# Four cross-attention layers on one core: denominators of the second layer by SBUF transfers, last block of the last layer in rows, and how banks and tokens are handed out

## The chip, the core and the metric

The kernel runs on one NeuronCore of a Trainium2 chip. The core has a matrix engine (TensorE, PE in the profile; its weight loads are PEld), a vector engine (VectorE, DVE), an activation engine (ScalarE, ACT), a general engine (GpSimd, POOL) and an engine that here only issues transfers (SyncE, SP). Each runs its own list of instructions in order; semaphores make one wait for another. Data lies in device memory (DRAM), in SBUF with 128 partitions, and in PSUM, eight banks of 2 KB per partition, which TensorE writes. The metric is the device time of one execution in microseconds (us), as the median of several runs.

## The reference

The input `x` has 2048 rows of 256 values, the context 1601 rows of 512. Four cross-attention layers follow each other: a masked one, a grouped one, two masked ones. Everything is float32.

```
masked layer (16 heads of 64):
  q = x @ Wq;  k = ctx @ Wk;  v = ctx @ Wv
  logits = q k^T / 8
  logits[:, tokens A] = bias -20*(1 - mask_A), tokens B alike     (added, four columns)
  x = x + softmax(logits) v @ Wo + bo
grouped layer (16 heads of 16, 4 heads of k and v):
  q = (x / rms(x) * norm_w) @ wq;  scores = q k^T / 4
  x = x + softmax(scores) v @ wo
```

## The kernel before

**Tiles.** Rows of x come in 4 batches (b) of 512, the 1601 context rows in 13 chunks (c) of up to 128. `xs` holds x transposed (256 features as 2 x 128 partitions, rows along the free side), so that it can be the moving side of projections. A masked layer has 8 blocks (n) of 2 heads, the grouped layer 4 blocks of 4 heads. A block with a batch is a unit; a unit has 13 steps, one per chunk. So there are 4 units in each block, 16 in the grouped layer and 112 in all.

**Steps.** The loop at the end goes through all steps two at a time. At one step three units are under way: one is scored (maxima are found), the one before is exponentiated (18 steps later), and its values are multiplied (20 steps later). The order of TensorE, DVE and ACT is the written one: at the end of the program every instruction of these is tied to the one before it. SP and POOL are ordered by the scheduler.

**Masked unit.** `masked_scores` computes scores transposed (keys on partitions), ACT copies them to a tile `p` in SBUF, DVE keeps a running maximum over chunks (L704). At the end of the scoring eight transposes and a reduction give the maximum of each row (L747, L748); it goes to DRAM and back, spread over all partitions (`on_all_partitions`), DVE subtracts it (L778), ACT exponentiates (L783), TensorE multiplies by v into `po` (L823), POOL adds the chunks up for the denominator (L788). `finish` sets the rest of the unit, in steps after its last value matmul: at 2 `denominators` (transposes of the sums L844, reduction L848, reciprocal L849, spread through DRAM), at 5 `divide` (POOL, L864), at 10 `project` (TensorE L872, and DVE adds to `xs`, with the bias in the last block of a layer).

**Grouped unit.** Scores are computed twice: rows first for the maxima only (`row_maxima`, L718, reduced by DVE, L731), then transposed (`scores_again`, L793) with the maximum as an extra row of q (row 16 of each quarter of 32 partitions; one column of v is 1, so that `oT` has the denominator in the same row). A step has two parts. In each, `grouped` takes two banks for maxima and two for scores, and issues maximum, score, maximum, score, which run beside each other on different rows of the array, then the values of another unit (L823). `finish` sets `denominators` at 3: four matmuls of `oT` with `den_rows` pick the denominator rows onto partitions (L853), DVE takes reciprocals (L856), the result goes to DRAM (`cols`, L655) and back spread over partitions (`by`, L658); at 5 `divide`, at 8 `project`.

**PSUM.** One bank for `po`, one (`pm`) for projections and small things, six for scores: as two pairs `s` and one pair `b` in masked stages, as six single banks `t` in the grouped one. The class `Scores` hands them out.

**Pieces.** Projections of the next block's keys and values, queries, and what `finish` sets are pieces, each with a cost. Set pieces run at their step; others fill in by a credit that each step earns.

**Start and end.** Token numbers are loaded to all partitions (L147), and DVE works out from them the order in which context rows are gathered, so that the four special rows come last (`key_order`); POOL gathers them (L258). The mask is loaded with one value per piece (L301, L302). After the last block's `project` of a batch, `rows_out` transposes `xs` back (L631), ACT and DVE copy half each (L634, L635), and two DMAs write it out.

Of the kernel before, what the change touches and what calls it, by code (L numbers as in the profile page):

```python
# [34 lines left out]
def tile_cross_attention_stack(ctx: ExitStack, tc: tile.TileContext, t: dict, out: bass.AP):  # L35
# [47 lines left out]
    NP = 22  # L83
    const = ctx.enter_context(tc.tile_pool(name="const", bufs=1))
# [15 lines left out]
    class Scores:  # L100
# [22 lines left out]
        def heads(self, three):  # L123

            if self.banks:
                return [self.banks.tile([P, 1, QB], FP, name="t") for _ in range(2)]
            self.turn += 1
            return [self.b() if three and self.turn % 3 == 0 else self.pair()]
# [13 lines left out]
    def token_numbers():  # L142

        idx = const.tile([P, NTOK], I32, name="tok_idx")
        for l, name in enumerate(masked_names):
            for s, which, queue in ((0, "A", nc.sync), (2, "B", nc.scalar)):
                queue.dma_start(  # L147
                    out=idx[:, 4 * l + s : 4 * l + s + 2],
                    in_=t[name + "token_indices_" + which]
                    .rearrange("(o s) -> o s", o=1).to_broadcast((P, 2)),  # L150
                )
        tok = const.tile([P, NTOK], FP, name="tok")
        nc.vector.tensor_copy(tok, idx)
# [144 lines left out]
    def masks_parts():  # L298
        masks = probs.tile([P, 2, NQ], FP, name="p")
        with nc.allow_non_contiguous_dma(reason="2048 values of a mask, once"):  # L300
            nc.sync.dma_start(out=masks[:, 0, :], in_=t["mask_S_fk1"].rearrange("(n p) -> p n", p=P))  # L301
            nc.sync.dma_start(out=masks[:, 1, :], in_=t["mask_S_fk0"].rearrange("(n p) -> p n", p=P))  # L302
        parts = const.tile([P, 6, NQ], FP, name="mask_parts")

        def make():
            nc.vector.tensor_scalar(masks, masks, -1.0, 1.0, ALU.mult, ALU.add)
# [59 lines left out]
    den_rows = const.tile([P, 4], FP, name="den_rows")  # L366
# [3 lines left out]
    def small_constants():  # L370
        with nc.allow_non_contiguous_dma(reason="columns of 256 values"):
            for name in masked_names:
                bo_of.append(const.tile([P, NC], FP, name="bo_" + name))
                nc.gpsimd.dma_start(out=bo_of[-1], in_=t[name + "bo"].rearrange("(k p) -> p k", p=P))
            nc.gpsimd.dma_start(out=normw, in_=t["L1_xattn_norm_w"].rearrange("(k p) -> p k", p=P))
        nc.gpsimd.memset(sel, 0.0)
        for h, r in enumerate(QUARTERS):
            nc.gpsimd.tensor_copy(den_rows[:, h : h + 1], ident[:, r + 16 : r + 17])
# [3 lines left out]
        nc.vector.tensor_reduce(one_row, den_rows, AX.X, ALU.add)  # L382
# [243 lines left out]
    def rows_out(b):  # L626
# [621 lines left out]
```

## Time and profile before

| | |
|---|---|
| median of 3 runs | 4831.26 us (4831.16 to 4831.56) |
| the profiled execution | 4829.9 us; its span 4828.2 us |
| PE busy | 4667.0 us (97%) |
| DVE busy | 3746.8 us (78%) |
| ACT busy | 3225.1 us (67%) |
| POOL busy | 2991.6 us (62%) |
| mean granted TensorE clock | 0.981 |

The profile is of one execution. A row of a timeline has the start in us from the span's start, the duration, the engine, the line of the code, what it writes and reads, and in brackets how long the engine was idle before and what ended that. The chain of waits goes back from the last instruction, at each step to what released it or to the instruction before it on its engine, so its shares say which engine's work the time consists of. The granted clock is the share of its full clock that TensorE was given; in this trace it is either 1.0 or 0.5 at any moment. A busy TensorE isn't TensorE at its peak, as the ends of matmuls are modelled.

The grouped layer's values, and with them L853, run from about 1449 to 2340 us. Its steps alternate little:

```profile
1599.74 0.40 PE L823 MATMUL po<-p,v 128*32 128x256 f32 x4
1600.07 0.18 PEld L718 LDWEIGHTS t<-kT,q 32*128 32x128 f32 x1 [0.41 <-DVE row_top L731]
...
1601.14 0.64 PE L823 MATMUL po<-p,v 128*32 128x256 f32 x8
...
1603.03 0.64 PE L823 MATMUL po<-p,v 128*32 128x256 f32 x8
...
1604.66 0.64 PE L823 MATMUL po<-p,v 128*32 128x256 f32 x8
```

These are rows of the timeline. The value matmuls of following parts start 1.89 and 1.63 us apart; between them lie the four matmuls of maxima and scores.

### The profile page before, as it was taken

The numbers are of one execution on the slowest core, as the hardware profiler recorded it, in microseconds if no ns is written. First come the engines' busy times: TensorE is split into PE (matmuls) and PEld (weight loads), VectorE is DVE, ScalarE is ACT, GpSimd is POOL, SyncE is SP. The second block draws the span as 40 slices with busy tenths as digits, with TensorE's granted clock in tenths as the row PEclk, the third lists the DMA queues.
The fourth block names the chain that finished last, engine by engine and source line by source line (L and its number), as shares of the span: only waits on it lengthen the run. The fifth ranks groups of instructions, "written<-read, shape, count | busy, mean of one in ns | idle before, by whom it ended". The sixth has DMA issues, their size and how long they took to land.

```text
span 4828.2 us, 64072 instructions
## 1 busy us (share of the span) xinstructions
PE 4667.0 (97%) x24020; PEld 1949.9 (40%) x24020; DVE 3746.8 (78%) x3766; ACT 3225.1 (67%) x4010; POOL 2991.6 (62%) x1440
## 2 busy tenths in 40 slices
PE   8999999999999999999999999999999999999996
PEld 5444444443433333343444444444444444444432
DVE  5888888888766666652678888888888888888886
ACT  5777777777545555544677777777777777777774
POOL 3777777778620000000577777777777777777787
PEclk9999999999889999998999999999999999999998
DMA  5322322222210000021232322322232222223201
GB/s 156 85 80 79 88 74 85 83 81 78 66 33 22 26 21 21 23 56 29 67 97 74 85 83 83 84 80 84 75 92 74 85 79 85 81 79 89 72 29 35
DMA packets 345990, 337.75 MB, mean 70 GB/s; under 512 B 112425, under 2 KB 301353, under 8 KB 345680
## 3 DMA queue, kind: packets, MB, share of 16 engines
q1 hardware_dynamic: 341984, 328.28, 23.8%
q8 instruction: 189, 3.10, 0.3%
q0 software_dynamic: 1152, 3.28, 0.2%
q10 hardware_dynamic: 2544, 2.10, 0.1%
q14 instruction: 121, 0.99, 0.1%
HBM read 318.76 MB, written 14.69 MB: 69 GB/s over the span
## 4 chain that ended last, share of the span: by engine, by line
PE 87%; DVE 10%; issue 1%; POOL 1%; ACT 1%; DMA 0%; POOLq 0%; ACTq 0%; DVEq 0%; SPq 0%
PE po L823 28%; PE s L687 20%; PE t L718 9%; PE pm L394 7%; PE pm L440 6%; PE s L872 4%; PE pm L464 4%; DVE ntop L748 2%; DVE rden L848 2%; PE s L844 2%; DVE xs L884 2%; PE s L747 2%; DVE top L704 1%; POOL sums L788 1%; PE t L793 1%
## 5 line engine op out<-in xcount | busy, mean ns | idle before, releaser
L788 POOL TENSOR_TENSOR sums<-sums,p 128x1024 f32<-128x1024 f32 (+1 forms) x1152 | 2726.4, 2367 | 741.0 <-ACT p L783 569.9
L699 ACT COPY p<-s 128x1024 f32<-128x1024 f32 (+1 forms) x1248 | 1234.7, 1014 | 665.7 <-PE s L687 573.5
L823 PE MATMUL po<-p,v 128*64 128x512 f32 (+3 forms) x8320 | 1506.7, 528 | 8.8 <-ACT p L783 5.8
L778 DVE TENSOR_TENSOR p<-p,b 128x1024 f32<-128x1024 f32 (+1 forms) x1248 | 1461.3, 1209 | 55.2 <-ACT b L773 52.9
L704 DVE TENSOR_TENSOR top<-s,top 128x1024 f32<-128x1024 f32 (+1 forms) x1056 | 1291.1, 1223 | 239.7 <-ACT p L699 176.7
L687 PE MATMUL s<-q,kT 64*128 64x512 f32 (+1 forms) x4992 | 1342.9, 632 | 82.9 <-DVE ntop L748 23.8
L783 ACT ACTIVATE p<-p 128x1024 f32<-128x1024 f32 (+1 forms) x1248 | 1254.8, 1057 | 49.1 <-DVE p L778 47.7
L823 PEld LDWEIGHTS po<-p,v 128*64 128x64 f32 (+3 forms) x8320 | 366.9, 126 | 1138.9 <-issue 905.4
L687 PEld LDWEIGHTS s<-q,kT 64*128 64x128 f32 (+1 forms) x4992 | 390.2, 182 | 721.1 <-issue 217.1
L805 ACT ACTIVATE p<-t 128x512 f32<-128x512 f32 (+1 forms) x760 | 413.7, 594 | 337.3 <-PE t L793 300.5
L731 DVE TENSOR_REDUCE row_top<-t 128x1 f32<-128x512 f32 x700 | 451.2, 686 | 215.7 <-PE t L793 186.6
L864 POOL TENSOR_TENSOR oT<-oT,by 128x512 f32<-128x512 f32 x112 | 142.9, 1276 | 719.4 <-DMA by<-cols 427.0
L793 PE MATMUL t<-q,kT 32*128 32x512 f32 (+1 forms) x1520 | 496.6, 656 | 0.0
L718 PE MATMUL t<-kT,q 32*128 32x512 f32 (+1 forms) x1880 | 490.1, 563 | 0.0
L394 PEld LDWEIGHTS pm<-wv,ct 128*128 128x128 f32 (+1 forms) x2600 | 300.4, 187 | 131.0 <-issue 68.4
L394 PE MATMUL pm<-wv,ct 128*128 128x128 f32 (+2 forms) x2600 | 333.3, 281 | 2.2 <-ACT v L398 0.9
L440 PE MATMUL pm<-ct,wk 128*128 128x256 f32 (+1 forms) x1344 | 314.5, 377 | 1.1 <-ACT ct L273 1.1
L748 DVE TENSOR_REDUCE ntop<-s 128x8 f32<-128x1024 f32 x96 | 117.6, 1225 | 232.8 <-PE s L747 232.8
L440 PEld LDWEIGHTS pm<-ct,wk 128*128 128x128 f32 x1344 | 230.8, 190 | 156.5 <-issue 101.0
L718 PEld LDWEIGHTS t<-kT,q 32*128 32x128 f32 x1880 | 183.7, 187 | 161.0 <-issue 94.1
L872 PE MATMUL s<-oT,wo 128*128 128x512 f32 x392 | 199.1, 631 | 15.1 <-POOL oT L864 11.1
L786 POOL COPY sums<-p 128x1024 f32<-128x1024 f32 x96 | 99.7, 1038 | 176.0 <-ACT p L783 176.0
(152 smaller groups left out, 2310.3 us busy)
## 6 DMA issues: line engine op xcount, KB each, us to landing
ct<-ctxT SPq DMA_DIRECT2D x288, 512.0 KB
xT<-xT SPq DMA_DIRECT2D x100, 512.0 KB
spread<-cols SPq DMA_DIRECT2D x96, 512.0 KB
by<-cols SPq DMA_DIRECT2D x192, 128.0 KB
xT<-xs SPq DMA_DIRECT2D x16, 512.0 KB
ct<-ctxT SPq DMA_DIRECT2D x48, 130.0 KB
wk<-in_L_xattn_Wk_dram SPq DMA_DIRECT2D x24, 256.0 KB
wv<-in_L_xattn_Wv_dram SPq DMA_DIRECT2D x24, 256.0 KB
```

The source lines that it names most:

```text
L394: nc.tensor.matmul(pv[:md, d, :f], ct(k)[:, d * P : d * P + md], wv[:, k, :], start=(k == 0), stop=(k == NCT - 1),)
L440: nc.tensor.matmul(pk, u.wk[:, k, :], ct(k), start=(k == 0), stop=(k == NCT - 1))
L687: nc.tensor.matmul(s[:m, h, :], self.u.kT[r, a : a + m], self.q[r, :], start=True, stop=(a != TAIL),)
L699: nc.scalar.copy(p[:m], s[:m])
L704: nc.vector.tensor_tensor(self.top[:m], s[:m], self.top[:m], ALU.max)
L718: nc.tensor.matmul(s[:, at : at + n], self.q[r, ts(q, P)], self.u.kT[r, a : a + n], start=True, stop=True,)
L731: nc.vector.tensor_reduce(self.top[:, of, q, k : k + 1], s, AX.X, ALU.max)
L778: nc.vector.tensor_tensor(self.p[c][:m], self.p[c][:m], self.less[:m], ALU.add)
L783: nc.scalar.activation(p[:m], p[:m], AF.Exp)
L788: nc.gpsimd.tensor_tensor(self.sums[:m], self.sums[:m], p[:m], ALU.add)
L793: nc.tensor.matmul(s[:m], self.u.kT[r, a : a + m], self.q[r, :], start=True, stop=True)
L823: nc.tensor.matmul(to, v, p, start=(c == 0 and not part), stop=(c == NT - 1 and part != 0))
```

## The change

- `Scores.heads` takes the number of kinds that are wanted at once; `grouped` asks for maxima and scores together and deals the four tiles out in turn.
- Token numbers are loaded to one partition, and a matmul with ones puts them onto all. The mask is loaded in rows and transposed by TensorE. The bias and norm columns are set to zero on DVE before their DMAs.
- In the grouped layer `den_columns` replaces the four matmuls: four DMAs take rows 16, 48, 80 and 112 of `oT` to a tile with 4 values on each of 128 partitions. They are set at step 1; `denominators` (now reciprocal and spread only) at 3, `divide` at 6, `project` at 8.
- In the last block of the last layer x is transposed into rows early (`rows_of_x`, at fixed steps), and `project_rows` computes rows of the output from `oT` (as weights) and `wo`, adds them and writes them out. The bias of the last layer is added one block earlier.
- The very last unit: POOL adds up only the first 6 chunks (`LAST_ADDED`); the others and POOL's sum are summed on TensorE by ones, onto all partitions (`self.dens`). x goes into PSUM beforehand as a matmul with the identity (`x_below`), the projection accumulates on it, and `quarters` takes reciprocal, division, projection, copy and output by quarters of 128 rows. It also runs the projection of the unit before.

```diff
-        def heads(self, three):
+        def heads(self, three, kinds=1):
             if self.banks:
-                return [self.banks.tile([P, 1, QB], FP, name="t") for _ in range(2)]
-            self.turn += 1
-            return [self.b() if three and self.turn % 3 == 0 else self.pair()]
+                tiles = [
+                    self.banks.tile([P, 1, QB], FP, name="t") for _ in range(2 * kinds)
+                ]
+                return [tiles[i::kinds] for i in range(kinds)]
...
-        idx = const.tile([P, NTOK], I32, name="tok_idx")
+        idx = probs.tile([1, NTOK], I32, name="p")
...
-                    .rearrange("(o s) -> o s", o=1).to_broadcast((P, 2)),
-                )
+                    in_=t[name + "token_indices_" + which].rearrange("(o s) -> o s", o=1),
+                )
+        row = probs.tile([1, NTOK], FP, name="p")
+        nc.vector.tensor_copy(row, idx)
+        pt = ps_m.tile([P, NTOK], FP, name="pm")
+        nc.tensor.matmul(pt, ones[:1, :], row, start=True, stop=True)
...
-            nc.sync.dma_start(out=masks[:, 0, :], in_=t["mask_S_fk1"].rearrange("(n p) -> p n", p=P))
...
+            nc.sync.dma_start(
+                out=rows[m * NQ : (m + 1) * NQ, :], in_=t[name].rearrange("(n p) -> n p", p=P)
+            )
...
+            nc.tensor.transpose(
+                pt.rearrange("p m n -> p (m n)"), rows, ident[: 2 * NQ, : 2 * NQ]
+            )
...
-    def rows_out(b):
+    def rows_of_x(b):
         pt = psum.pair((QT, C))
         for q in range(QT):
             for k in range(NC):
                 nc.tensor.transpose(pt[:, q, ts(k, P)], xs[:, b, k, ts(q, P)], ident)
...
+        x_rows_of[b] = work.tile([P, QT, C], FP, name="ct", bufs=3)
+        nc.scalar.copy(x_rows_of[b], pt)
...
-            else:
+            elif c < self.added:
                 nc.gpsimd.tensor_tensor(self.sums[:m], self.sums[:m], p[:m], ALU.add)
...
+            if self.masked and self.very_last:
+                if c == 0:
+                    self.dens = ps_m.tile([P, QB], FP, name="pm")
+                todo = [self.p[c]] if c >= self.added else []
+                if c == NT - 1:
+                    todo.append(self.sums)
+                for p in todo:
+                    k = m if p is self.p[c] else P
+                    for h in range(2):
+                        nc.tensor.matmul(
+                            self.dens[self.rows(h), :], ones[:k, :64], p[:k, h, :],
+                            start=(c == self.added), stop=(p is self.sums),
+                        )
...
             else:
-                pd = ps_m.tile([P, QT, 4], FP, name="pm")
-                for q in range(QT):
-                    nc.tensor.matmul(
-                        pd[:, q, :], self.oT[:, columns(q)], den_rows, start=True, stop=True
-                    )
-                nc.vector.reciprocal(rden, pd.rearrange("p q h -> p h q"))
+                nc.vector.reciprocal(rden, self.dens)
...
+        def den_columns(self):
+            self.dens = small.tile([P, 4, QT], FP, name="dens", bufs=1)
+            with nc.allow_non_contiguous_dma(reason="512 values, four at a time"):
+                for h, r in enumerate(QUARTERS):
+                    nc.sync.dma_start(
+                        out=self.dens[:, h, :],
+                        in_=self.oT[r + 16 : r + 17, :].rearrange("o (p q) -> o p q", q=QT),
+                    )
...
+        def project_rows(self, py=None):
+            py = py or psum.pair((QT, C))
+            for q in range(QT):
+                nc.tensor.matmul(
+                    py[:, q, :], self.oT[:, ts(q, P)], self.u.wo, start=True, stop=True
+                )
+            rows = x_rows_of[self.b]
+            nc.vector.tensor_tensor(rows, py, rows, ALU.add)
+            for q in (0, QT // 2):
+                rows_out(self.b, rows, q, QT // 2)
...
+        def quarters(self, before):
+            rden = work.tile([P, NC, QB], FP, name="xT")[:, 0, :]
+            for q in range(QT):
+                nc.vector.reciprocal(rden[:, ts(q, P)], self.dens[:, ts(q, P)])
+                nc.gpsimd.tensor_tensor(
+                    self.oT[:, ts(q, P)], self.oT[:, ts(q, P)], rden[:, ts(q, P)], ALU.mult
+                )
+            before.project_rows(psum.b().rearrange("p a (b c) -> p (a b) c", c=C))
+            rows = work.tile([P, QT, C], FP, name="ct", bufs=3)
+            for q in range(QT):
+                nc.tensor.matmul(
+                    self.py[q], self.oT[:, ts(q, P)], self.u.wo, start=False, stop=True,
+                )
+                nc.scalar.copy(rows[:, q, :], self.py[q])
+                rows_out(self.b, rows, q, 1)
...
+            if not self.masked:
+                return [
+                    (1, Piece(self.den_columns, 0.0)), (3, Piece(self.denominators, 0.0)),
+                    (6, Piece(self.divide, 0.0)), (8, Piece(self.project, 2.0, False)),
+                ]
...
+            for b, at in enumerate((2, 12, 38, NB * NT + 12)):
+                piece = Piece(lambda b=b: rows_of_x(b), 1.0, False)
+                if b == NB - 1:
+                    piece = Piece(lambda: of[len(units) - 1].x_below(), 2.0, False)
+                pieces.at(start + at, [(0, piece)])
...
-                tops = psum.heads(three) if scoring else []
-                exps = psum.heads(three) if exping else []
+                tiles = psum.heads(three, bool(scoring) + bool(exping))
+                tops = tiles.pop(0) if scoring else []
+                exps = tiles.pop(0) if exping else []
```

## The prediction

> **What bounds it now.** First the page's chain of waits that ended last: 87% of the span is TensorE, and no single line leads.
>
> ```profile
> ## 4 chain that ended last, share of the span: by engine, by line
> PE 87%; DVE 10%; issue 1%; POOL 1%; ACT 1%; DMA 0%; POOLq 0%; ACTq 0%; DVEq 0%; SPq 0%
> ```
>
> The change touches four stretches, so I read the chain for each. In the second layer (cut to 1450–2120 us) it is TensorE throughout: no other engine has more than 0.1%, and L853, the denominators' matmul, holds 3.5%:
>
> ```profile
> by line: PE t L718 52.9%; PE po L823 27.7%; PE t L793 4.8%; PE pm L576 3.7%; PE pm L853 3.5%; PE t L872 3.4%; PE pm L440 1.9%; PE pm L546 1.4%; issue 0.3%; PE pm L761 0.3%; ACT kT L550 0.1%
> ```
>
> The same chain in order of time, 1510–1532 us, has start, us and what. L853 stands between one value matmul and the next maxima, and costs TensorE 1.96 us:
>
> ```profile
> 1516.71 0.57 PE po L823 x8
> 1517.28 1.96 PE pm L853 x8
> 1519.24 0.62 PE t L718
> ```
>
> Windows around it (stretch, length, PE busy, granted clock, DMA share, GB/s) show a second price: the 4 us after it run at 0.57 of the clock.
>
> ```profile
> 1516.00:1520.00 4.00, 4.00 (x32) 1.00 0.00 0
> 1520.00:1524.00 4.00, 4.00 (x28) 0.57 0.11 15
> 1524.00:1528.00 4.00, 4.00 (x46) 1.00 0.17 56
> ```
>
> Last the chain of the end, which is a row of engines waiting for each other:
>
> ```profile
> 4806.29 2.00 PE s L844 x8
> 4808.31 1.24 DVE rden L848
> ...
> 4809.80 1.54 DMA cols<-rden
> ...
> 4811.90 3.10 DMA by<-cols
> ...
> 4816.48 3.79 PE s L872 x4
> ...
> 4821.76 1.77 PE s L631 x7
> ...
> 4824.17 0.69 DVE ct L635
> ```
>
> **Banks in turn: nothing.** In steady state one part takes TensorE 1.64 us, the next 1.89 us; the 0.26 us between are a maximum waiting for DVE to empty the bank of three maxima before. The change hands out the four banks in another order of the names. But a bank is bound at a tile's first write, in TensorE's order, and that order (maximum, score, maximum, score) stays. Built, both programs keep maxima in banks 2, 3, 4 and scores in 5, 6, 7, and each waits for the same earlier reader. I cost it at 0.
>
> **Denominators without TensorE.** Removed: 16 units x four matmuls (eight instructions each) of 1.96 us. The chain holds 23.5 us of them at 12 units (3.5% of 670 us) and 2.0 us for the one at 2258; the last (2335 us) runs into the third layer, where DVE is also late, and I don't count it: 15 x 1.96 = 29.4 us.
>
> The clock: 7 of the 16 L853 (at 1462, 1517, 1628, 1736, 1897, 2121, 2183 us) are followed within 1.9 to 3.5 us by exactly 3.4 us of half clock; otherwise TensorE is busy there. The Trainium skill ("TensorE: Matmul & The Clock Gate", What's actually happening) has free-running windows of 3.41 us and halves the clock after an idle one. By the rule as stated, L853 costs no clock, since TensorE isn't idle for a window: 29.4 us in all. By the row a window that is largely filled with 4-column matmuls counts as idle. I take the row. From L853 to L853 a unit lasts 52.2 to 54.2 us without a dip and 53.6 to 57.3 with one; I take 1.2 us a dip (half of 3.4 us less slack), 7 x 1.2 = 8.4 us.
>
> Added: four DMAs on SP per unit (2 KB each, 128 pieces of 16 bytes), from SBUF to SBUF. They wait for oT, copied at 1503.9–1504.5 us. Behind them on SP stand the next unit's xT and factor loads, the 1/denominator's own cols and by, and the top rows; xT is needed a unit (50 us) later. The reciprocal stays at step 3 of the unit after, behind that step's maxima, i.e. at about 1516.48 + 1.29 = 1517.8 us. **Cover: 13.3 us.** No row shows such a transfer; the nearest is cols<-rden, the same 16-byte pieces in one DMA:
>
> ```profile
> SPq L658 <- DMA cols<-rden: 36.4, 16, 2.8
> ```
>
> That is 36.4/16 = 2.3 us on average, 2.8 at most. Issuing four costs about 1.7 us (the four by<-cols), so they land some 4 us after oT. The skill speaks against it: "DMA: Bandwidth & Descriptors" (Rules for kernel authors) wants many small transfers coalesced, and its fixed cost is about 2 us each; served one after the other that is 8 us plus the issue, 10 us, still inside 13.3. Both give 0; the ends are 0 and a stall (third rival). Division moves from step 5 to 6 and projection stays at 8: cols and by took until 1526.3, projection came at 1542.4, so the 3.5 us later divide is hidden. The piece's cost going from 1 to 0 moves later keys' pieces forward, with the same work.
>
> **Start: 0.6 us.** Token numbers come as 8 bytes per DMA instead of 128 copies of them, landing before 7.6 us (they then waited 5.85 us); a matmul and two small copies are added. DVE's 6.5 us of index work and the first gathers move up by 2 to 3 us. But TensorE is then still transposing x: in the trace L592 ends at 20.3 us and the two halves of the first context block came at 20.26 and 21.12 us, so only about 0.8 us is there to win, less 0.2 us for the mask's transpose (L631 needs 1.09 us for eight). Ends: -1 and +2.5. The two mask DMAs with 4-byte pieces held SP 4.1 us; row loads replace them. The bias loads move from POOL's first 6 us to about 80 us, behind four DVE memsets: four issues, 3.2 us on POOL, whose next work (L786) starts at 90.85; free.
>
> **Last block: 2 us.** There DVE is the bound (busy 35.8 of 40 us; 13 subtractions and maxima of 1.21 us and five small ones make 36.4 of a unit of about 37). For x in rows, ACT copies it earlier (1.01 us) and DVE adds once (1.21) where it had two adds (1.41) and a copy (0.69): 0.9 us for each of the first two batches. TensorE's transposes and 1024 projected columns only move. The bias goes into the block before, +0.2 us of DVE under TensorE.
>
> **End: 22.5 us.** From the trace's rows:
> - The last unit's exponentials no longer wait in the middle for the copy out and for the unit before's sums after five chunks; those sums come after seven. The copy of the spread maxima is at about 4767.2 (4768.97 before: no wait of 1.9 us for L879), chunk 6's exponential ends at 4779.1 (1.12 us each), and the sums' transposes at 4779.3.
> - TensorE: values of chunks 5 and 6 (1.94), ones for 6 (0.97, as values), x into PSUM (16 instructions as L394's, 1.8), six chunks of 0.97 + 0.97 (11.6), ones for the tile into which POOL has added chunks 0 to 5 (0.97): 4796.6. POOL's six chunks are done by 4783.
> - Four reciprocals of 128x128. Not in the trace: 4 elements take 178 ns (L617), 8 take 203 (L849), so 6.3 ns an element and 0.96 us each; lower bound 0.2, an ordinary DVE pass. I take 0.96: 4800.4. Then POOL 0.45 (line through 128x512 and 128x1024), TensorE 0.48, ACT 0.37: 4801.7. The other batch's 1.93 us projection lies beneath.
> - Last copy before: 4824.86. Gain 23.2; I take 22.5 for SP's six output issues in a row. With everything at half clock, as the end is now (26 us from 4804), it would be about 11; with fast reciprocals 25.
>
> **Sum.** 29.4 + 8.4 + 0.6 + 2 + 22.5 = 63 us. Profiled execution 4829.9 (span 4828.2) → 4767; the median of the runs is 1.4 us above it: **4768 us**.
>
> **Rivals.**
> 1. Four small DMAs just fail the cover: the reciprocal holds DVE's maxima about as long as the matmul held TensorE. Then 63 - 38 = 25 us: 4806. For it: nothing measured lands 128 pieces on 128 partitions from one row. Against: 13.3 us of cover. 6%.
> 2. The turn of banks removes the 0.26 us stall in all 208 steps: 54 us more, 4714. Against: same banks in both builds. 2%.
> 3. **Slower**: the four transfers are served one at a time at the dearest row for 128 small pieces, the token loads' 5.85 us. They land at 23.4 us, DVE stands 10.1 us at the reciprocal in each of 16 units, TensorE with it: +162 - 63 = +99, 4930. It decides from a landing of 13.3 + 63/16 = 17.2 us after oT. Against: those 5.85 us lay beside 2 MB of x. 4%.
> 4. The end gains half: TensorE falls to half clock while waiting for reciprocals, or x in PSUM holds both pairs too long: 4780 to 4785. 10%, inside my range.
>
> **Numbers.** Forecast with its own spread 78%, rivals 1 to 4 as above. Upward: no clock gain (+8.4), end 11 (+11.5), start -1: 4790; toward rival 1 I go to 4803. Downward: all 16 L853 and 1.7 us a dip (-5.5), end 25, start +2.5: 4758; I go to 4750. What counts as no change is within 0.2%, about 10 us. Faster 0.93, same 0.02, slower 0.05.
>
> **What would show it.** Right: L853 gone from the second layer's chain, fewer half-clock stretches, no DVE wait at its reciprocal for dens, unit spacing near 51.5 us; steps still alternating 1.64 and 1.89 us. From the last unit's final sum on TensorE to the end about 8 us. Wrong: DVE or SP waiting on dens; the dips elsewhere instead; reciprocals far from 0.96 us.

## The result, and the profile after

| | before | after |
|---|---|---|
| median | 4831.35 us (4831.16 to 4831.56) | 4754.41 us (4745.24 to 4755.4) |
| ratio | | 0.9837 (95%: 0.9822 to 0.9853) |
| the profiled execution | 4829.9 us | 4745.2 us |
| mean granted TensorE clock | 0.981 | 0.992 |
| half clock in the span | 185 us | 72 us |

The changed kernel is 77 us faster in the median; 63 us were forecast (4768 us), and the result lies inside the range of 4750 to 4803 us. Its profiled execution is 9 us quicker than its other three, so the difference of the two profiles is 84.7 us.

The page's chain of waits, after:

```profile
## 4 chain that ended last, share of the span: by engine, by line
PE 87%; DVE 10%; issue 1%; ACT 1%; POOL 0%; DMA 0%; another core or an unknown queue 0%; ACTq 0%; DVEq 0%; POOLq 0%
```

The kernel is bound as before. The chain in the second layer (1450 to 2110 us of after) has no denominators any more (3.5% before):

```profile
by line: PE t L744 54.4%; PE po L849 28.4%; PE t L819 5.2%; PE pm L595 3.8%; PE t L920 3.5%; PE pm L459 1.9%; PE pm L565 1.4%; PE pm L413 0.8%; issue 0.3%; PE pm L787 0.3%
```

L744, L849 and L819 are the former L718, L823 and L793. Windows of 4 us around the reciprocal, which runs at 1515.6 us in after (stretch, length, PE busy, PEld, DVE, ACT, POOL busy, granted clock, DMA share, GB/s):

```profile
1512.00:1516.00 4.00, 4.00 (x40) 1.19 (x32) 2.93 (x6) 2.20 (x5) 0.00 (x0) 1.00 0.00 1
1516.00:1520.00 4.00, 4.00 (x34) 1.43 (x34) 2.58 (x4) 2.32 (x5) 0.00 (x0) 1.00 0.18 28
1520.00:1524.00 4.00, 4.00 (x42) 1.59 (x42) 2.58 (x4) 2.97 (x6) 1.27 (x1) 1.00 0.13 44
```

The clock column stays at 1.00 where it fell to 0.57 before. Rows of the timeline of after, value matmuls:

```profile
1588.11 0.64 PE L849 MATMUL po<-p,v 128*32 128x256 f32 x8
1590.00 0.64 PE L849 MATMUL po<-p,v 128*32 128x256 f32 x8
1591.64 0.64 PE L849 MATMUL po<-p,v 128*32 128x256 f32 x8
```

They still alternate 1.89 and 1.64 us: the turn of banks took no stall away. VectorE never stands at its reciprocal of the transferred denominators: the view of tile `dens` lists nothing under "sat idle".

```profile
L894 DVE RECIPROCAL rden<-dens x16: 243/243/245, 1464.3 to 2277.7; 128x16 f32<-128x16 f32 x16
its engine sat idle before it (us, times) until:
```

Last the end of after, timeline rows from the last sums by ones on:

```profile
4731.96 1.03 PE L862 MATMUL pm<-sums,ones 128*64 128x512 f32 x4
...
4733.03 3.39 DVE L961 RECIPROCAL xT<-pm 128x128 f32<-128x128 f32 x4 [7.83 <-PE pm L862]
...
4735.78 4.23 SPq L658 DMA_DIRECT2D out_dram<-ct  x6
...
4738.26 0.37 ACT L971 COPY ct<-s 128x256 f32<-128x256 f32 x1 [0.85 <-PE s L968]
```

A reciprocal of 128x128 takes 3.39 / 4 = 0.85 us (0.96 was taken); from the end of the sums to the span's end (4743.5) are 10.5 us, some 8 were forecast.

**Where the time went.** As marks I take the reduction that ends each unit's search for maxima (units from 0: 0–31 first layer, 32–47 second, 48–79 third, 80–111 last). From mark to mark, with the half clock that the trace's clock records have in between:

| from mark to mark | before | after | gain |
|---|---|---|---|
| start to unit 0 | 75.8 (0 half) | 82.3 (6.8 half) | -6.5 |
| unit 0 to 33, with the change to the second layer | 1339.6 (61.4 half) | 1334.7 (47.8 half) | 4.9 |
| 33 to 47: second layer | 786.1 (37.5 half) | 747.6 (10.2 half) | 38.5 |
| 47 to 48: change to the third layer | 87.4 (34.1 half) | 70.9 (0 half) | 16.5 |
| 48 to 107 | 2321.8 (17.1 half) | 2313.7 (3.4 half) | 8.1 |
| 107 to 111: last block | 148.1 (0 half) | 149.0 (0 half) | -0.9 |
| 111 to the end | 69.4 (34.3 half) | 45.3 (3.4 half) | 24.2 |

(Gains are taken before rounding. The 48-to-107 row loses its half clock within the first four units, as the third layer begins.)

### The profile page after: what moved, and what is told of

Read it like the earlier page. It is cut to its first block, busy times and chain, and to the rows that moved or that the text cites. A ratio compares the mean times of both kernels' runs of the same rounds, so it can differ in the third digit from the quotient of the medians.

```text
span 4743.5 us, 64047 instructions
## 1 busy us (share of the span) xinstructions
PE 4596.3 (97%) x23943; PEld 1914.1 (40%) x23943; DVE 3744.2 (79%) x3768; ACT 3226.5 (68%) x4013; POOL 2977.4 (63%) x1436
## 4 chain that ended last, share of the span: by engine, by line
PE 87%; DVE 10%; issue 1%; ACT 1%; POOL 0%; DMA 0%; another core or an unknown queue 0%; ACTq 0%; DVEq 0%; POOLq 0%
PE po L849 28%; PE s L713 20%; PE t L744 9%; PE pm L413 7%; PE pm L459 6%; PE pm L483 4%; PE s L920 4%; DVE rden L891 2%; PE s L887 2%; DVE ntop L774 2%; DVE xs L932 2%; PE s L773 2%; DVE top L730 1%; DVE p L804 1%; PE t L819 1%
## 5 line engine op out<-in xcount | busy, mean ns | idle before, releaser
L814 POOL TENSOR_TENSOR sums<-sums,p 128x1024 f32<-128x1024 f32 x1145 | 2711.0, 2368 | 736.8 <-ACT p L809 566.0
L849 PE MATMUL po<-p,v 128*64 128x512 f32 (+3 forms) x8320 | 1493.5, 522 | 4.9 <-ACT p L809 2.6
L713 PE MATMUL s<-q,kT 64*128 64x512 f32 (+1 forms) x4992 | 1336.7, 629 | 85.9 <-DVE ntop L774 23.2
L849 PEld LDWEIGHTS po<-p,v 128*64 128x64 f32 (+3 forms) x8320 | 365.7, 125 | 1115.8 <-issue 889.3
L819 PE MATMUL t<-q,kT 32*128 32x512 f32 (+1 forms) x1520 | 489.1, 643 | 0.0
L744 PE MATMUL t<-kT,q 32*128 32x512 f32 (+1 forms) x1880 | 481.9, 553 | 0.0
L744 PEld LDWEIGHTS t<-kT,q 32*128 32x128 f32 x1880 | 182.5, 185 | 163.1 <-issue 96.7
L799 ACT COPY b<-spread 128x1024 f32<-128x1024 f32 x96 | 97.5, 1015 | 150.9 <-DVE p L804 150.0
L920 PE MATMUL s<-oT,wo 128*128 128x512 f32 x376 | 187.4, 621 | 2.8 <-DVE row_top L757 1.7
```

The costliest lines, as they stand in the source:

```text
L713: nc.tensor.matmul(s[:m, h, :], self.u.kT[r, a : a + m], self.q[r, :], start=True, stop=(a != TAIL),)
L744: nc.tensor.matmul(s[:, at : at + n], self.q[r, ts(q, P)], self.u.kT[r, a : a + n], start=True, stop=True,)
L814: nc.gpsimd.tensor_tensor(self.sums[:m], self.sums[:m], p[:m], ALU.add)
L819: nc.tensor.matmul(s[:m], self.u.kT[r, a : a + m], self.q[r, :], start=True, stop=True)
L849: nc.tensor.matmul(to, v, p, start=(c == 0 and not part), stop=(c == NT - 1 and part != 0))
```

## The experiments

Each is timed beside the kernel before on its own chip; the medians of before there lay between 4826.6 and 4836.1 us, so ratios are compared. A profile shows one execution, and not always a typical one; where it was the fastest or the slowest of its run, that is said.

### Each part alone

**Only the turn of banks.** `heads` and `grouped` as changed, all else as before.

```diff
-                tops = psum.heads(three) if scoring else []
-                exps = psum.heads(three) if exping else []
+                tiles = psum.heads(three, bool(scoring) + bool(exping))
+                tops = tiles.pop(0) if scoring else []
+                exps = tiles.pop(0) if exping else []
```

> The kernel before with only the turn of the single banks changed. My theory: the banks are bound in TensorE's order, which stays, so the program is the same: 4831.4 us, within 1 us of before, and steps of the second layer still alternate 1.64 and 1.89 us. Rival (the prediction's second): the turn takes away the 0.26 us stall in each of 208 steps: 54 us less, 4777 us.

Measured: ratio 1.0001 (0.9992 to 1.0009). The second layer takes 783.4 us from mark to mark, 2.7 less than in before, with two of before's short stretches of half clock (dips, 3.41 us each) missing. The time shows no change: this part does nothing.

**Only the denominators.** `den_columns`, the reciprocal from `self.dens`, and the new steps and costs.

```diff
+                    (1, Piece(self.den_columns, 0.0)), (3, Piece(self.denominators, 0.0)),
+                    (6, Piece(self.divide, 0.0)), (8, Piece(self.project, 2.0, False)),
-                (2 if self.masked else 3, Piece(self.denominators, 1.0, not self.masked)),
-                (5, Piece(self.divide, 0.0)), (last, Piece(self.project, 2.0, False)),
```

> The kernel before with only the second layer's denominators by SBUF transfers (with their new steps and costs). My theory after seeing the two traces: all of the gain between the 33rd and the 56th unit belongs to this part, 42 us in the second layer and 20 to 25 us at the change to the third layer: 62 to 67 us, so 4764 to 4769 us. Rival A: as the prediction had it, 29.4 us of TensorE and 8.4 us of clock, 38 us: 4793 us; the gain at the change of layers then comes from another part or from chance. Rival B (the clock has nothing to do with it): 29 us, 4802 us.

Measured: ratio 0.9881 (0.9867 to 0.9896), that is 57.5 us. The second layer takes 747.6 us and the change to the third 70.9 us with no half clock, both to 0.1 us as in after. As the third layer begins it has 17 us of half clock where after's first profile has 3.4, and is 5 us longer there, which is most of what it lacks to 62. (The fastest of its four executions was profiled.) Rival A (38 us) falls.

**Only the last block and unit.** Rows of x early, `project_rows`, `x_below`, `quarters`, `LAST_ADDED = 6`.

```diff
+            if self.very_last:
+                return [(0, Piece(lambda: self.quarters(of[len(units) - 2]), 2.0))]
```

> The kernel before with only the last block and the last unit changed (x in rows early, rows of the output, the last unit's denominator by TensorE, quarters). My theory: the end gains the 24 us that the two traces show and the last block about nothing, 24 us: 4807 us. Prediction as made: 2 + 22.5 = 24.5 us. Rival: the warm end of the one profiled execution was luck, in other executions TensorE falls to half clock at the end, and the gain is some 9 us less: 4816 us.

Measured: ratio 0.9959 (0.9944 to 0.9973), 19.8 us. In its profile the last mark to the end takes 44.9 us (in seven profiles with the old end it takes 68.6 to 70.6, in seven with the new one 44.9 to 45.3), so the end gains 24 to 25 us, and the cold end that the rival expected is seen in none: the old ends have 31 to 41 us of half clock, the new ones 0.4 to 3.6. What each of the moved pieces brings was not taken apart. The last block before it takes 151.7 us, 3.6 more than in before, with 6.8 us of half clock. Such a stretch costs both kernels: 148.1 us without and 152.0 or 152.1 with one of 10.2 us in the old block, 149.0 and 153.0 in the new. Its executions lie at 4812, 4813, 4820 and 4821 us; only the 4812 was profiled, so where the two longer ones lost it is open.

**Only the start.** Tokens by a matmul, mask in rows, columns set to zero first, bias loads later.

```diff
-        nc.vector.tensor_copy(tok, idx)
+        pt = ps_m.tile([P, NTOK], FP, name="pm")
+        nc.tensor.matmul(pt, ones[:1, :], row, start=True, stop=True)
+        nc.vector.tensor_copy(tok, pt)
```

> The kernel before with only the start changed (tokens by a matmul, mask loaded in rows, constants set to zero first, bias loads later). My theory: this part costs the 5 to 6.5 us by which the first units come later in the new trace, as TensorE waits at about 25 us and then runs at half clock: 4836 to 4838 us. Prediction as made: 0.6 us less, 4830.8 us. Rival: the loss at the start of the one profile was chance, and the times scatter by several us around before's.

Measured: ratio 0.9997 (0.9988 to 1.0006): no change that could be told, between 5.8 us faster and 2.9 us slower. My theory of a loss of 5 us and more falls. The run with only the turn of banks, whose instructions are those of before, has the same stall and comes to unit 0 at 84.6 us instead of 75.8. Rows of its timeline:

```profile
29.48 0.37 ACT L449 COPY kT<-pm 128x256 f32<-128x256 f32 x1 [6.39 <-remote]
29.91 2.54 PE L700 MATMUL s<-q,kT 64*128 64x512 f32 x8 [3.90 <-issue]
```

ACT stands 6.39 us at something that the trace doesn't name, TensorE 3.9 us behind it, and 6.8 us of half clock follow. Seven of the fourteen profiles have such a remote wait, of 4.6 to 7.3 us. Old and new start both have it. Among the experiments it goes with the chip: three of the four profiles on this run's chip have it (the fourth has a wait of 8.5 us that is put down to nothing) and all three on another, none of the five on two further chips. Of the first pair, before has none and after has one. Unit 0 comes at 83.8 to 84.9 us with the old start on this chip, and at 75.9 to 77.6 on a chip without the wait. On this chip, the only one in the experiments with profiles of both starts, the new start comes to unit 0 at 81.8 us, 2.0 to 3.1 us earlier than the old ones; that is one profile, and the whole time does not show it. What ACT waits for was not found.

### The denominators: matmul, order, clock

**New order, old matmuls.** The piece costs and steps of the change, with the four matmuls left in.

```diff
-                (2 if self.masked else 3, Piece(self.denominators, 1.0, not self.masked)),
-                (5, Piece(self.divide, 0.0)), (last, Piece(self.project, 2.0, False)),
+                    (3, Piece(self.denominators, 0.0)),
+                    (6, Piece(self.divide, 0.0)), (8, Piece(self.project, 2.0, False)),
```

> The kernel before with its four matmuls for the denominators kept at step 3, but with the new costs and steps (denominators cost 0 instead of 1, division at step 6 instead of 5), so that pieces come in the new order. My theory: order alone moves no work off TensorE: 0, within 3 us of before, and the change from the second to the third layer keeps 40 to 55 us of half clock. Rival: the 16 us by which that change of layers got shorter come from the new order of the pieces: 16 to 20 us faster.

Measured: ratio 1.0014 (1.0007 to 1.0021), 7 us slower by the ratio and 3.6 in the medians, outside the 3 us that I allowed. Its profile, of the slowest of 20 executions, has 55 us of half clock in the second layer (37.5 in before) and 44 at the change of layers. The rival falls: order alone brings nothing. Why there are more dips in the second layer is worked out under the wide denominators below.

**Old order, no matmuls.**

```diff
+                    (1, Piece(self.den_columns, 0.0)), (3, Piece(self.denominators, 1.0)),
+                    (5, Piece(self.divide, 0.0)), (8, Piece(self.project, 2.0, False)),
```

> The kernel before with the denominators by SBUF transfers, but with the old costs and steps (denominators cost 1 at step 3, division at 5), so that the pieces stay in the old order. My theory: it gains as much as the whole part did, 55 to 60 us, since the matmuls themselves are what costs: 38 us in the second layer and 16 us at the change to the third. Rival: 38 us only, and the rest belongs to the order of the pieces. A division that waits for its spread denominator at step 5 would show as a wait of POOL only, and cost nothing.

Measured: ratio 0.991 (0.9891 to 0.9929), 43.5 us. In its profile the second layer gains 37 us, but the change to the third layer stays long (86.8 us). This is the slowest of its four executions, 8 us above their median; the other three were not profiled. Windows of 30 us there, first of before, then of this run, then of after:

```profile
2235.00:2265.00 30.00, 29.25 (x124) 9.21 (x120) 4.60 (x5) 12.54 (x13) 0.00 (x0) 0.60 0.02 3
2265.00:2295.00 30.00, 27.15 (x144) 8.29 (x146) 6.12 (x5) 13.92 (x15) 1.26 (x1) 0.83 0.07 21
2295.00:2325.00 30.00, 26.22 (x139) 8.09 (x139) 6.94 (x6) 11.84 (x13) 0.00 (x0) 0.72 0.06 22
```

```profile
2196.00:2226.00 30.00, 28.17 (x114) 7.66 (x116) 5.14 (x6) 12.10 (x14) 1.27 (x1) 0.60 0.06 10
2226.00:2256.00 30.00, 27.15 (x140) 8.45 (x140) 6.51 (x6) 14.49 (x15) 0.00 (x0) 0.83 0.02 6
2256.00:2286.00 30.00, 26.22 (x140) 7.62 (x137) 6.35 (x6) 11.35 (x13) 0.00 (x0) 0.72 0.08 30
```

```profile
2175.00:2205.00 30.00, 27.25 (x175) 7.93 (x176) 8.57 (x7) 18.64 (x20) 0.00 (x0) 1.00 0.11 36
2205.00:2235.00 30.00, 26.88 (x175) 8.23 (x172) 6.28 (x6) 18.56 (x19) 1.26 (x1) 1.00 0.04 10
2235.00:2265.00 30.00, 24.92 (x161) 7.83 (x159) 9.61 (x8) 13.36 (x14) 0.00 (x0) 0.94 0.11 36
```

The clocks of before and of this run are the same, 0.60, 0.83, 0.72, though one has the matmuls and the other not. So taking the matmuls away does not by itself make this stage warm, and neither does the new order (44 us above). With both it had no half clock in four profiles (only the denominators, after twice, and the early reciprocal below), but 10.2 and 21.3 us in the two with wide sums of squares further below, and there TensorE's list of matmuls in this stage is the same as after's, one for one. So the list doesn't settle it.

Over thirteen profiles without the fillers of the last run the length from mark 47 to 48 goes with the half clock in it: 70.9 to 71.6 us at none, 75.7 at 10.2, 80.2 at 21.3, 83.5 at 23.9, 86.8 at 34.1, 91.6 at 44.4, some 0.44 to 0.53 us for each us of half clock. At the same 34.1 us of half clock the stage takes 87.4 us with the one matmul group that falls into it (before) and 86.8 without (this run). So all but some 0.6 us of this stage's 16.5 us goes with the clock. Why it is warm in one execution and cold in another is not settled.

**Wide denominators.** Before, but each of the four matmuls writes its four columns 32 times.

```diff
-                pd = ps_m.tile([P, QT, 4], FP, name="pm")
+                pd = ps_m.tile([P, QT, 32, 4], FP, name="pm")
-                        pd[:, q, :], self.oT[:, columns(q)], den_rows, start=True, stop=True
+                        pd[:, q], self.oT[:, columns(q)],
+                        den_rows.rearrange("p (o h) -> p o h", o=1).to_broadcast((P, 32, 4)),
+                        start=True, stop=True
```

> The kernel before, but its four matmuls for the denominators write 128 columns (the same four, 32 times) instead of 4 each: more columns on TensorE, the same instructions. My theory: the half clock after these matmuls comes from windows with little column work in them, so that with 128 columns the stretches of 3.4 us after them go, at no more time for the matmuls, as these wait for their weights: 8 us faster, and more if the change to the third layer keeps its clock too. Rival A: only idle time counts for the clock, and the stretches have another cause: no change, or slower by up to 16 times 1 us as there are more columns. Rival B: what counts is something else in these matmuls (their strided weights): the stretches stay.

Measured: ratio 0.9978 (0.9971 to 0.9985), 10.6 us faster with 32 times the columns. The matmuls, by form (min, median, max ns), in before and then in this run:

```profile
L853 PE MATMUL pm<-den_rows,oT x128: 374/374/397, 1462.5 to 2336.9; 128*128 128x4 f32 x128
```

```profile
L853 PE MATMUL pm<-den_rows,oT x128: 397/397/602, 1463.3 to 2324.5; 128*128 128x128 f32 x128
```

Four columns take 374 ns, 128 columns 397. The matmuls start every 0.24 and 0.25 us, hardly slower than their weight loads (every 0.23 us), so both go at the pace of their weights. In the chain a group costs 2.06 us, where it cost 1.96:

```profile
1516.75 2.06 PE pm L853 x8
```

The windows around this group in this run:

```profile
1514.00:1518.00 4.00, 4.00 (x34) 2.20 (x30) 2.58 (x4) 2.17 (x4) 0.00 (x0) 1.00 0.00 0
1518.00:1522.00 4.00, 4.00 (x36) 1.81 (x35) 2.00 (x4) 1.50 (x3) 0.00 (x0) 1.00 0.07 2
1522.00:1526.00 4.00, 4.00 (x46) 1.38 (x40) 3.04 (x6) 2.64 (x6) 0.00 (x0) 1.00 0.25 70
```

No dip is left between 1453 and 2227 us, where before has eight. Seven of before's eight are those that the prediction counted; TensorE counts as busy throughout the 3.41 us before each of them, so idle time isn't what fell in the wide run. The eighth (at 1534 us) is another matter: in the 3.41 us before it TensorE is idle for 0.78 us behind a copy, and the run "old order, no matmuls" has a dip (at 1526.4 us) behind the same wait without any of these matmuls. In before, then in that run:

```profile
1533.39 0.43 PE L546 MATMUL pm<-ks,sel 64*128 64x65 f32 x2 [0.78 <-ACT kT L550]
```

```profile
1525.82 0.43 PE L547 MATMUL pm<-ks,sel 64*128 64x65 f32 x2 [0.78 <-ACT kT L551]
```

Prices: the second layer takes 776.7 us, 9.4 less than in before, although its 14 groups cost 0.10 us more each. So eight dips (27.3 us of half clock) cost 9.4 + 1.4 = 10.8 us, 1.35 each. The two dips that the turn of banks lacked give the same, 2.7 us. Against after the layer is 29.1 us longer, 2.08 for each wide group; the narrow ones at 1.96 us make 27.4.

**Which groups are followed by a dip.** In each profile all stretches of half clock start on one grid of 3.413 us. A group of narrow matmuls lasts 2.03 us. Five profiles have them (before, only the turn, only the last block, only the start, new order), with 14 groups each between marks 33 and 47. Of these 70 groups, 39 have at least 1.92 us of their time within one window of the grid, and each of the 39 is followed by half clock in the next window. Another 28 have at most 1.77 us in one window, and none of them is. Of the three between (1.79 to 1.91), one is. In the wide run five groups have over 2 us in one window, and none is followed by half clock. So how many dips an execution has depends on where its groups fall on the grid: 7, 5, 7, 10 and 11 of 14 in these profiles. The dips of the last two often come 54.6 us apart, which is 16 windows, so that the next group falls on the same place again; that is how one execution comes to more dips than another. It is not the order: the run with only the start, in the old order, has 10.

### The cover of the transfers

**Reciprocal at step 1**, right behind the transfers.

```diff
-                    (1, Piece(self.den_columns, 0.0)), (3, Piece(self.denominators, 0.0)),
+                    (1, Piece(self.den_columns, 0.0)), (1, Piece(self.denominators, 0.0)),
```

> The changed kernel, but with the reciprocal of the second layer's denominators at step 1, right behind the transfers that bring them, instead of step 3: the cover shrinks from 12 us after the first issue to some 5. My theory: the last packet of the four transfers ends 3.6 us after the first issue, 4.5 to 5.5 in four units, and the semaphore comes 1 to 2 us later, so VectorE waits 0 to 1.5 us per unit: 0 to 15 us slower than the changed kernel. Rival (the prediction's third, transfers served one by one): 10 us and more of wait per unit, over 100 us slower.

Measured: ratio 0.9824 (0.9808 to 0.984), after on the same chip 0.9837: no slower. VectorE does wait now (tile dens: its instructions, what its engine waited for, in us and times):

```profile
L894 DVE RECIPROCAL rden<-dens x16: 243/253/255, 1457.4 to 2276.4; 128x16 f32<-128x16 f32 x16
its engine sat idle before it (us, times) until:
  DMA dens<-oT: 18.1, 11
  issue: 1.2, 1
who waited for it (us, times):
  DVE rden L894: 18.1, 11
  PEld t L744: 6.1, 8
```

One of the eleven waits is 8.2 us long, in the change of layers where VectorE has nothing else; the rest are about 1 us each. A row of VectorE's timeline:

```profile
1559.14 1.29 DVE L757 TENSOR_REDUCE row_top<-t 128x1 f32<-128x512 f32 x2 [0.35 <-PE t L819]
1561.29 0.25 DVE L894 RECIPROCAL rden<-dens 128x16 f32<-128x16 f32 x1 [0.86 <-DMA dens<-oT]
```

This reciprocal starts 4.1 us after oT's copy ended; over the units it is 4.0 to 6.1 us, so all four transfers have landed by then. TensorE's weight loads wait 6.1 us for it in all (1.5 in after), and still the second layer takes 747.6 us as in after: waits of 1 us cost nothing here.

### The changed kernel again, and versions beyond it

**After once more**, on the chip of the run above and the next.

> The changed kernel itself once more, on the chip of the next two runs. My theory: the parts measured alone give the whole: 57 us from the denominators and 20 us from the last unit, 77 us, nothing from the start: a ratio of 0.984; and the change to the third layer has little half clock again (under 20 us). Rival: the 3.4 us of half clock at that change was chance of one execution, and 40 to 50 us are seen there this time, which costs up to 25 us.

Measured: 4754.9 us, ratio 0.9837 (0.9821 to 0.9854), as the parts give. Mark 47 to 48: 70.9 us with no half clock, then 17 us of it as the third layer begins (3.4 in the first profile), and 10.2 us in the last block; the two rows are 5.4 and 4.0 us longer, which is the difference between the first profile and the median.

**Wide sums of squares.** After, but the norm's matmuls (one column each) write 128 equal columns.

```diff
-            pt = ps_m.tile([P, QT], FP, name="pm")
+            pt = ps_m.tile([P, QT, 128], FP, name="pm")
-                        pt[:, q : q + 1], held["x"][:, k, columns(q)], ones[:, :1],
+                        pt[:, q, :], held["x"][:, k, columns(q)], ones[:, :128],
-            nc.vector.tensor_scalar(by, pt, 16.0 / C, 16.0 * EPS, ALU.mult, ALU.add)
+            nc.vector.tensor_scalar(by, pt[:, :, 0], 16.0 / C, 16.0 * EPS, ALU.mult, ALU.add)
```

> The changed kernel, but the sums of squares of the norm (16 instructions on TensorE with one column each, four times, at 1262, 1319, 1384 and 1440 us) write 128 equal columns instead of one. My theory, from the run with wide denominators: half clock follows narrow matmuls, so the stretches right after these four (3.4, 20.5, 6.8 and 10.2 us) go or get shorter, at no more time for the matmuls: half of 41 us at most, 10 to 20 us faster than the changed kernel. Rival A: the stage there is kept by VectorE (75 to 90% busy), TensorE's clock is slack: the stretches go and the time stays within 3 us. Rival B: idle time between the maxima makes these stretches, not the narrow matmuls: they stay.

Measured: 4743.9 us, ratio 0.9822 (0.9806 to 0.9839), 11 us below after's median on that chip, though one of its four executions (4755.0) lies among after's; by the ratios it is 7 us, and the intervals overlap. The second of the four groups with what stands before it, in after and then in this run:

```profile
1316.26 3.21 PE L744 MATMUL s<-kT,q 32*128 32x512 f32 x8 [3.20 <-DVE row_top L757]
1319.40 3.89 PE L629 MATMUL pm<-ones,xT 128*128 128x1 f32 x16
```

```profile
1310.43 3.21 PE L744 MATMUL s<-kT,q 32*128 32x512 f32 x8 [3.20 <-DVE row_top L757]
1313.57 4.00 PE L629 MATMUL pm<-ones,xT 128*128 128x128 f32 x16
```

Windows behind it, of after and then of this run:

```profile
1320.00:1324.00 4.00, 4.00 (x17) 3.50 (x18) 1.14 (x4) 0.20 (x1) 0.00 (x0) 0.50 0.00 0
1324.00:1328.00 4.00, 3.21 (x12) 0.52 (x8) 2.93 (x3) 2.67 (x3) 0.00 (x0) 0.50 0.15 28
1328.00:1332.00 4.00, 3.47 (x9) 1.34 (x10) 2.95 (x4) 1.20 (x2) 3.53 (x2) 0.50 0.18 38
```

```profile
1316.00:1320.00 4.00, 3.64 (x20) 1.88 (x18) 2.13 (x4) 1.51 (x3) 0.00 (x0) 0.90 0.02 1
1320.00:1324.00 4.00, 2.35 (x8) 0.60 (x8) 3.90 (x4) 2.56 (x3) 2.23 (x1) 0.95 0.37 66
1324.00:1328.00 4.00, 4.00 (x10) 1.49 (x10) 1.76 (x3) 0.00 (x0) 2.45 (x2) 0.62 0.00 0
```

The stretches at the first, third and fourth group (3.4, 6.8 and 10.2 us in after; the third begins 1.1 us into its group, the others near the end) are gone. The long one at the second does not begin with the narrow matmuls, as my expectation had it: in after it starts at 1316.5 us, 2.9 us before them and behind 3.20 us in which TensorE is idle, and lasts 20.5 us. In this run half clock comes behind the same wait (1309.9 us), but ends after 6.8 us, during the wide matmuls, and comes back once for 3.4. So the narrow matmuls draw it out; they don't start it. In all eleven profiles with the narrow form the window of the grid behind each of the four groups is at half clock (for 19 of the 44 half clock had begun before), in the three with the wide form at none.

From mark 30 to 33 half clock falls from 44 us to 17, and the stage from 172.6 to 164.0 us; with the fourth stretch gone the second layer falls from 747.6 to 744.4 us. Rival A is not borne out in these stages, though the whole time alone would not refute it. B falls for what follows the groups, and holds for where the long stretch begins. At the change to the third layer 10.2 us came back.

**The same once more.**

> The changed kernel with the wide sums of squares once more, as the candidate that beats both and as the one the next run is compared with. My theory: 4744 us where before is at 4834, a ratio of 0.982; the stage of the first change of layers keeps its clock again (under 20 us of half clock between 1255 and 1455 us), and executions differ by up to 10 us as other stretches of half clock come and go. Rival: the first result was luck, and the ratio comes back to the changed kernel's 0.984.

Measured: 4744.2 us, ratio 0.9827 (0.9813 to 0.984), with 27 us of half clock in marks 30 to 33, where I had expected under 20. The stage takes 168.6 us, the second layer 744.3. The interval overlaps with after's, and after was not timed on this chip, so medians can't be set side by side. The stages are shorter, by 4 to 9 us and by 3 us; that the whole is faster than after is likely, by some 5 to 10 us, but not shown.

**Fillers** on top of that: in the change to the third layer one more matmul behind each half step's values, adding zeros.

```diff
+            if filled and c < NT - 1:
+                nc.tensor.matmul(
+                    self.po[r.start : r.start + 15, at], u.v[:m, c, 17:32], p, start=False, stop=False
+                )
```

> The kernel of the run before, and in the change from the second to the third layer one more matmul behind each half step of values, with the zero columns of v as weights and 256 columns, which adds zeros to the sums. My theory: half clock in that stage (27 us of it between 2160 and 2260 us in the first wide run) comes from windows with too little column work, so it goes: 13 us to win, less what the 100 or so added matmuls of about 0.2 us put on TensorE's path; as TensorE is idle there for some 15% of the time only, half of their 20 us: 0 to 5 us faster. Rival: TensorE sets the pace there and the fillers are simply added, 10 to 20 us slower, with or without half clock.

Measured: 4747.7 us, ratio 0.9845 (0.9827 to 0.9862), not faster than the run without them (3.6 us slower in the medians, within the intervals). The first 60 us of the stage in this run:

```profile
2170.00:2200.00 30.00, 28.49 (x186) 8.91 (x186) 6.01 (x5) 16.54 (x17) 0.00 (x0) 1.00 0.07 19
2200.00:2230.00 30.00, 26.88 (x166) 8.59 (x163) 6.28 (x6) 15.76 (x17) 1.27 (x1) 1.00 0.04 10
```

The half clock is gone from the whole stage (21.3 us in the run without), but the stage takes 82.1 us where a warm one without fillers takes 70.9: the added matmuls stand on TensorE's path, as the rival said (though for less than its 10 to 20 us), and eat what they bring. (In the change to the second layer, where nothing was altered, it also met 10 us more of half clock than the run before.)

## Why the prediction held, and where it did not

- **Banks in turn, 0:** right.
- **Matmuls off TensorE, 29.4 us:** right. The 14 groups between marks 33 and 47 come to 27.4 us at the 1.96 us that the prediction read, and 29.1 us were measured for their wide form at 2.06 us. The 15th lies in the change to the third layer, where some 0.6 us of it can be seen.
- **Clock behind them, 7 x 1.2 = 8.4 us:** right, and a little low: 1.35 us a dip, 9.5 us for the seven. Which seven of the groups have one is a matter of the grid; other executions of the same matmuls had 5 to 11. Row and rule were weighed against each other here. By the Trainium skill ("TensorE: Matmul & The Clock Gate", What's actually happening) the clock falls after an idle window, so with TensorE busy the wide matmuls would have gained nothing; they gained 10.6 us in the whole time. The row decides.
- **The term that the sum does not have: clock at the change to the third layer.** The prediction counted the half clock behind the denominators' matmuls and put the rest at nothing, without a reason, though before has 51 us of it from 2237 to 2323 us (10.2, 13.7, 10.2, 17.1). The first profile shows a gain of 16.5 us there and 8.1 us where the third layer begins; the second profile, near the median, 16.5 and 2.7. That is more than the excess of 77 over 63; its last block, 4.9 us slower, takes some back. What starts the half clock there stays open. The range had no allowance for this term, so that 4754 us still lies above its lower end of 4750 is partly luck.
- **Cover of the transfers, 4 us after oT against 13.3:** right, 4.0 to 6.1 us. In after the reciprocal comes 12.1 to 14.2 us behind oT in 14 units and 7.0 and 9.0 in the last two, and VectorE waits in none, so the first rival falls too. The 10 us of the prediction's second working, with a fixed cost of about 2 us for each transfer from the Trainium skill ("DMA: Bandwidth & Descriptors", Anatomy of one DMA, a fit to transfers that GpSimd issues; these are issued by SP), are not what was measured. The third rival's price of 10 us per unit is refuted, and the run with the early reciprocal shows that even 1 us of wait costs nothing.
- **Start, 0.6 us:** neither shown nor refuted (1.5 us faster, between 5.8 faster and 2.9 slower). The 6.5 us lost in the first profile are not shown to be the new start's: on the chip of the experiments where both were profiled it came 2 to 3 us earlier.
- **Last block, 2 us:** wrong by 3: it is 0.9 us slower without any half clock. Which of its moved instructions takes the time was not tried.
- **End, 22.5 us:** 24.2. From the last mark, the final sums end at 34.7 us (37.9 were worked out, 4796.6 less 4758.7) and the last copy at 40.4 (66.1 before), a gain of 25.7 where 23.2 were taken; the output issues behind it then cost 1.5 us more than before, not 0.7. Half clock in the end falls from 34.3 to 3.4 us, which the forecast counted on; its fourth rival, a cold end, was seen in none of seven profiles.

## What to carry over

Price TensorE's clock from the whole trace, not only beside the instructions that change: a stage where TensorE is just underfed can hold more half clock than the change itself, and it can be warm or cold from one execution to the next with the same list of instructions. Where a matmul of few columns waits for its weights anyway, try more columns: they cost 0.10 us for a group of eight instructions here, and no dip followed. A small transfer with 13 us of cover needs no argument about its price; measure its landing once by moving its reader forward. And before one profile is read against another, look where its execution lies among the others.

## What was not expected of the hardware

- Half clock follows groups of narrow matmuls while TensorE counts as busy all the time. With 4 columns, 39 of 39 groups of 2.03 us that lie (all but at most 0.11 us) within one window of 3.41 us are followed by it; with 1 column, the window behind all 44 groups of 3.9 us is at half clock, in 19 of them from before. With 128 columns it was none of five and none of twelve.
- The stretches of half clock (but for those that outlast the program) are multiples of 3.41 us, and their starts within one execution lie such multiples apart (1257.7, 1308.9, 1336.2 and 1346.4 us in before: 15, 8 and 3 of them). What half clock costs is some 0.4 to 0.5 of its length, where TensorE is always busy (10.8 us for 27.3) as well as at the change of layers.
- ACT's wait of 4.6 to 7.3 us at about 25 us from the start is named as a remote wait, with the old and the new start alike.
